# Weighted values of two pieces in one run, and the first layers' narrow products behind them, in a two-layer perceiver block

## The chip, the cores and the metric

The kernel runs on one core of a Trainium2 chip. A core has a matmul engine (PE, with its weight loads listed as PEld), a vector engine (DVE), a scalar engine (ACT), a general engine (POOL) and a queue that issues transfers (SP). The time is the device time of one execution in microseconds; the kernel before took 2208.38 us (median of three runs, 2206.98 to 2210.51).

## The reference

32 sequences `x` of 64 tokens with 256 channels each go through two layers. Each has a cross part, an attention or recurrent part and a feed-forward part. The part that matters here is the cross attention of the second layer: every sequence looks at its own context of 1601 rows.

```python
q = _split_heads(query @ Wq.T + bq)          # 16 heads of 16 channels
k = _split_heads(bank @ Wk.T + bk)
v = _split_heads(bank @ Wv.T + bv)
scores = jnp.einsum('bhqd,bhkd->bhqk', q / score_scale, k)
attn = jax.nn.softmax(scores, axis=-1)
ctx = jnp.einsum('bhqk,bhkd->bhqd', attn, v)
```

The first layer ahead of it has a product with the context's mean, a self-attention over the 64 tokens (16 heads, with a bias by distance) and a routed feed-forward; behind it come a convolution, a recurrence, a gated feed-forward and a feed-forward with rounded weights. Everything is float32, apart from a few small helpers.

## The kernel before

Two sequences make a tile of 128 rows, so there are 16 positions (`NT`). A position's context is worked off in 13 pieces (`NU`): two sequences times two halves of the channels times three pieces of 512 keys, and one piece (number 9 of 0 to 12) with the 65 last keys of both sequences. With 16 positions that is 208 pieces. `split` and `scanned` (L636, L644) say which keys piece g is; in the row scores and the keys the 65 last come first.

For a piece, PE and the others do this:

- `keys` (L671): the key projection, tile `kps`, 128x512; ACT copies it to `kt` with a bias (L692).
- `row_scores` (L713): the scores of queries by keys, tile `r`, from 32-row slices of the array; DVE reduces each of two tiles to its maxima, `mx` (L732).
- `values` (L694): the value projection `vps`; DVE copies it to one of five tiles `vau` (L709).
- `column_scores` (L752): the same scores turned round, tile `s`, with the negated maxima added through a small product (L767, L773); ACT takes the exponential into `pt` (L779).
- `weighted` (L782): `pt` times the values, accumulated over the position in one PSUM tile `o` (L797). Each product fills 32 of the array's 128 columns, and four stand next to each other.

The pieces of one position follow each other in a loop over g (L1256), whose order is written out by hand (`manual_schedule`, L1212): what is emitted first is first in each engine's queue. The order of one turn is column scores of g, values of g+4, steps of place 0, row scores of g+5, weighted values of g, keys of g+6, steps of place 1. The two score tiles of `row_scores` and the two of `column_scores` share one pool (`ps_sc`, two buffers of two banks, L57 to L66), so the column scores of the next turn take the tiles that `mx` reads. All other products share three one-bank buffers (`ps_mm`, `mm_tile`).

The other layers are generators that yield between steps. `Steps` (L1111) holds one with a stretch of turns and a number of steps, and `run(t, place)` (L1128, called from L1248) takes the steps that are due. Plans of place 3 (the first layers, `layer0`, and the second layers) run a step at place 0 if the generator last yielded `ACT`, and at place 1 otherwise. In `layer0` (L262) the products concerned are the values `v_ps` (L319, two slices of 64 columns) and the summed values `summed_values` (L381 to L388, four slices of 32 columns), which need the transposed weights `tpp` (`weights`, L369) copied to `pT` by ACT (L376).

SP loads a sequence's context into `ctxT` (two buffers) at pieces 2 and 9 of each position (L1261).

Of the kernel before, what the change touches and what calls it, by code (L numbers as in the profile page):

```python
# [9 lines left out]
F32 = mybir.dt.float32  # L10
# [5 lines left out]
P = 128  # L16
NB = 32
S = 64
# [3 lines left out]
NT = NB * S // P  # L22
# [5 lines left out]
PIECE = 512  # L28
NP = L // PIECE
TAIL = L - NP * PIECE  # L30
NU = 4 * NP + 1
# [13 lines left out]
def perceiver_kernel(ctx: ExitStack, tc: tile.TileContext, a: dict, out: bass.AP):  # L45
# [13 lines left out]


    ACT = "ACT"

    def sc_tile(name):
        return ps_sc.tile([P, 2, 512], F32, tag="sc", name=name)
# [197 lines left out]
    def layer0(ti, csum, k=0, soon=False):  # L262
# [47 lines left out]
        for oc in range(2):  # L310
            nc.gpsimd.tensor_tensor(  # L311
                kbd[oc], kT[:, oc, :].rearrange("p (b k) -> p b k", b=2).unsqueeze(2).to_broadcast([P, 2, 4, S]),
                mask4.unsqueeze(1).unsqueeze(3).to_broadcast([P, 2, 4, S]), ALU.mult)
        yield ACT
        v_ps = mm_tile([P, 2, P], f"v0_{ti}")
        for b in range(2):
            for c in range(2):
                for h in range(2):
                    nc.tensor.matmul(v_ps[h * S:(h + 1) * S, b, :], lhsT=xT[:, c, b * S:(b + 1) * S],  # L319
                                     rhs=w_v[:, c, :].rearrange("p (a h d) -> p h a d", h=2, d=16)[:, h],  # L320
                                     start=(c == 0), stop=(c == 1))
        for h in range(2):
            nc.scalar.copy(vbd[k][h * S:(h + 1) * S, :, :, h, :],
# [50 lines left out]
            return t  # L374

        def weights_out(oc, t):  # L376
            pT = tile_([P, 4, P], "pT", f"pT{oc}")
            nc.scalar.copy(pT, t)
            return pT

# [8 lines left out]

        pT = weights_out(0, weights(0))  # L390
        yield ACT
        t = weights(1)
        summed_values(0, pT)
        pT = weights_out(1, t)
        yield ACT
        summed_values(1, pT)
        yield
        o = mm_tile([P, D], f"wo_{ti}")
        mm2(o, lambda c: oT[:, c, :], lambda c: w_o[:, c, :])
# [271 lines left out]
    def keys(g):  # L671

        pos, h, k = scanned(g)
        if h is None:
            w = wholes[pos]
            w.kt = big.tile([P, 4, TAIL], F32, tag="ktr", name=f"ktr_{w.ti}", bufs=2)
            o = mm_tile([P, 2, 2 * TAIL], f"kps_{w.ti}")
            for oc in range(2):
                mm2(o[:, oc, :], lambda c: w_k2[:, c, oc * P:(oc + 1) * P],
                    lambda c: w.rest[:, c].rearrange("p b l -> p (b l)"))  # L680
            for oc in range(2):
                nc.scalar.activation(w.kt.rearrange("p (b o) l -> p o b l", o=2)[:, oc],
                                     o[:, oc, :].rearrange("p (b l) -> p b l", b=2), AF.Identity,
                                     bias=chv[:, oc, BK2:BK2 + 1])
            return
        hf = halves[h]
        kt = big.tile([P, PIECE], F32, tag="kt", name=f"kt_{hf.name}_{k}", bufs=7)
        hf.kt.append(kt)
        o = mm_tile([P, PIECE], f"kps_{hf.name}_{k}")
        cT = ctxs[hf.batch]  # L690
        mm2(o, lambda c: w_k2[:, c, hf.oc * P:(hf.oc + 1) * P], lambda c: cT[:, c, k * PIECE:(k + 1) * PIECE])
        nc.scalar.activation(kt, o, AF.Identity, bias=chv[:, hf.oc, BK2:BK2 + 1])  # L692
# [59 lines left out]
    def column_scores(g):  # L752

        pos, h, k = split(g)
        w, qbd = wholes[pos], queries[pos]
        ps = [sc_tile(f"s_{g}_{m}") for m in range(2)]
        kr = TAIL if h is None else P
        for i in range(4):
            r = slice(32 * i, 32 * i + 3)
            o = ps[i // 2][:kr, i % 2, :]  # L760
            if h is None:

                for q in range(4):
                    nc.tensor.matmul(o[:, q * P:(q + 1) * P], lhsT=onesb[r, :kr], rhs=halves[4 * pos + q].neg[r, :],
                                     start=(q == 0), stop=False)
            else:
                nc.tensor.matmul(o, lhsT=onesb[r, :], rhs=halves[h].neg[r, :].unsqueeze(1).to_broadcast([3, 4, P]),  # L767
                                 start=True, stop=False)
        for j in range(4):
            q = j if h is None else h % 4  # L770
            for i in range(4):
                r = slice(32 * i, 32 * i + 32)
                nc.tensor.matmul(ps[i // 2][:kr, i % 2, j * P:(j + 1) * P],  # L773
                                 lhsT=w.kt[r, j, :] if h is None else halves[h].kt[k][r, j * P:(j + 1) * P],
                                 rhs=qbd[r, q % 2, q // 2].rearrange("p h q -> p (h q)"), start=False, stop=(j == 3))
        w.pt[g] = []
        for m in range(2):
            pt = big.tile([P, 2, 4, P], F32, tag="pt", name=f"pt_{g}_{m}", bufs=2)
            nc.scalar.activation(pt[:kr].rearrange("p i k c -> p i (k c)"), ps[m][:kr], AF.Exp)  # L779
            w.pt[g].append(pt)  # L780

# [329 lines left out]
    class Steps:  # L1111

        def __init__(self, gen, t0=0, t1=1, n=1, place=0):
            self.gen, self.t0, self.t1, self.n, self.place, self.done = gen, t0, t1, n, place, 0
            self.kind = None
# [7 lines left out]
                    self.gen = None  # L1126

        def run(self, t, place):  # L1128
            at = place if self.place == 2 else self.place
            if self.place == 3:  # L1130
                if (self.kind == ACT) != (place == 0):
                    return
                at = place
            if at == place:
                now = t + (0.5 * place if self.place >= 2 else 0)
                while self.gen is not None and self.done * (self.t1 - self.t0) <= (now - self.t0) * self.n:
                    self.step()
                    if self.place == 3:
                        break

        def all(self):
            while self.gen is not None:
# [69 lines left out]
    with tc.manual_schedule(engines={ET.PE, ET.DVE, ET.Activation, ET.Pool}):  # L1212
        ahead, beside, summing = Steps(first()), Steps(first_layer(1, 1)), Steps(early_sums())
        early = [lambda g=g: keys(g) for g in range(1, 4)] + [lambda: keys(0)] + [
            lambda g=g: values(g) for g in range(4)] + [lambda g=g: keys(g) for g in range(4, 6)]

        def others():
            if 0 in csums:
                summing.step()
            if 1 in csums:  # L1220
                beside.step()

        ahead.step()
        late = [late_weights]
        while 0 not in queries:
            if early:
                early.pop(0)()
            ahead.step()
            others()
            if 1 in csums and late:  # L1230
                late.pop()()
        for f in early + late:
            f()
        for g in range(4):
            row_scores(g)
            others()
        maxima(0)
        row_scores(4)
        others()
        maxima_rows(0)  # L1240
        if beside.gen is not None:
            plan.insert(0, Steps(beside.gen, 0, 3, 30 - beside.done, 2))
        planned(biased(), 3, 5, 2, 1)
        if summing.gen is not None:
            plan.insert(0, Steps(summing.gen, 0, 5, 12, 0))
        planned(all_ternary(), 5, 23, 24, 2)

        def run(t, place):  # L1248
            for s in [s for s in plan if s.t0 <= t]:
                s.run(t, place)  # L1250
                if t >= s.t1 and t < NU * NT - 1:
                    s.all()
                if s.gen is None:
                    plan.remove(s)

        for g in range(NU * NT):  # L1256
            pos, p = divmod(g, NU)
            if pos + 1 < NT:
                if p == 0:
                    wholes[pos + 1].rest = load_rest(order[pos + 1])  # L1260
                if p in (2, 9):  # L1261
                    load_batch(2 * pos + 2 + p // 8)
            column_scores(g)
            if g + 4 < NU * NT:
                values(g + 4)
            if p == 0 and pos:
                normalise(pos - 1, 3)
            elif p > 3 * NP:
                normalise(pos, p - 3 * NP - 1)
            if g + 4 < NU * NT and scanned(g + 4)[2] == NP - 1:  # L1270
                maxima_rows(scanned(g + 4)[1])
            run(g, 0)
            if g + 5 < NU * NT:
                row_scores(g + 5)
                if scanned(g + 5)[2] == NP - 1:
                    maxima(scanned(g + 5)[1])
            weighted(g)
            if g + 6 < NU * NT:
                keys(g + 6)
            if p == 1 and pos:  # L1280
                x4[pos - 1] = projected(pos - 1)
            run(g, 1)
        normalise(NT - 1, 3)
        x4[NT - 1] = projected(NT - 1)
        plan.append(Steps(second_layer(NT - 1)))
        while plan:
            for s in list(plan):
                s.step()
                if s.gen is None:
                    plan.remove(s)  # L1290
# [47 lines left out]
```

## Time and profile before

| | |
|---|---|
| median of the runs | 2208.38 us |
| the profiled execution | 2210.8 us, span 2209.1 us |
| from the first column scores of the loop to the last | 91.7 to 2126.2 us |
| PE busy from 100 to 2126 us | 1961.6 of 2026 us, granted clock 0.99 |
| DVE, ACT, POOL busy in the same stretch | 1259.9, 857.1, 280.6 us |
| first 100 us: PE busy | 68.1 us, granted clock 0.78 |
| last 79 us: PE busy | 44.9 us, granted clock 0.66 |

The profile is that of one execution. Its rows give an instruction's start and length in microseconds, the engine, the line of the kernel, what it writes and reads and how many are merged into the row; in brackets the engine's idle time just before and what ended it. A matmul's record is longer than its share of the array's time, because matmuls follow each other before the first has ended, so the distance from start to start is what counts. Listed waits of an engine give the total, the number of times and the longest.

### The profile page before, as it was taken

The numbers are of one execution on the slowest core, as the hardware profiler recorded it, in microseconds if no ns is written. First come the engines' busy times: TensorE is split into PE (matmuls) and PEld (weight loads), VectorE is DVE, ScalarE is ACT, GpSimd is POOL, SyncE is SP. The second block draws the span as 40 slices with busy tenths as digits, with TensorE's granted clock in tenths as the row PEclk, the third lists the DMA queues.
The fourth block names the chain that finished last, engine by engine and source line by source line (L and its number), as shares of the span: only waits on it lengthen the run. The fifth ranks groups of instructions, "written<-read, shape, count | busy, mean of one in ns | idle before, by whom it ended". The sixth has DMA issues, their size and how long they took to land. (4 is left out here: it accounts for less than half of the span.)

```text
span 2209.1 us, 69768 instructions
## 1 busy us (share of the span) xinstructions
PE 2077.7 (94%) x31887; PEld 1520.5 (69%) x31903; DVE 1342.9 (61%) x2686; ACT 907.4 (41%) x1397; POOL 315.5 (14%) x525
## 2 busy tenths in 40 slices
PE   6799999999999999999999999999998899999984
PEld 4567677677676777777776776777776566677763
DVE  4556765666656566665665656565667656656554
ACT  3334444444435344444544444353433234334342
POOL 2111111111211111111111111111100000000011
PEclk8799999999999999999999999999999999999986
DMA  7223221111212111111211111101100101000000
GB/s 263 87 100 112 80 77 64 64 52 34 70 66 73 64 53 64 37 67 63 76 52 64 66 34 66 64 34 41 37 32 34 42 31 34 14 32 35 2 4 5
DMA packets 46175, 126.41 MB, mean 57 GB/s; under 512 B 12558, under 2 KB 28344, under 8 KB 45880
## 3 DMA queue, kind: packets, MB, share of 16 engines
q1 hardware_dynamic: 45320, 121.13, 16.0%
q8 instruction: 250, 4.10, 0.8%
q10 hardware_dynamic: 560, 0.81, 0.1%
q14 instruction: 45, 0.37, 0.1%
HBM read 119.83 MB, written 2.10 MB: 55 GB/s over the span
## 5 line engine op out<-in xcount | busy, mean ns | idle before, releaser
L779 ACT ACTIVATE pt<-s 128x1024 f32<-128x1024 f32 (+1 forms) x416 | 403.1, 1021 | 307.9 <-PE s L773 307.7
L732 DVE TENSOR_REDUCE mx<-r 128x2 f32<-128x1024 f32 x384 | 452.2, 1220 | 114.3 <-PE r L725 113.9
L233 PE MATMUL vps<-w_L_xattn_WvT,ctxT 128*128 128x128 f32 x3072 | 397.7, 283 | 0.0
L233 PE MATMUL kps<-ctxT,w_L_xattn_WkT 128*128 128x512 f32 x768 | 382.9, 622 | 11.4 <-DMA ctxT<-ctxT 11.4
L692 ACT ACTIVATE kt<-kps,chv 128x512 f32<-128x512 f32 x192 | 131.9, 687 | 636.7 <-PE kps L233 636.7
L709 DVE COPY vau<-vps 128x512 f32<-128x512 f32 (+1 forms) x208 | 143.3, 689 | 399.5 <-PE vps L233 399.5
L233 PEld LDWEIGHTS vps<-w_L_xattn_WvT,ctxT 128*128 128x128 f32 x3072 | 361.6, 193 | 24.1 <-issue 3.4
L797 PEld LDWEIGHTS o<-pt,vau 128*32 128x32 f32 (+1 forms) x13312 | 197.7, 111 | 150.9 <-issue 144.2
L797 PE MATMUL o<-pt,vau 128*32 128x64 f32 (+1 forms) x13312 | 232.3, 222 | 4.2 <-ACT pt L779 4.2
L725 PE MATMUL r<-kt,qbd 32*128 32x512 f32 x1536 | 228.5, 652 | 2.4 <-DVE mx L732 1.5
L233 PEld LDWEIGHTS kps<-ctxT,w_L_xattn_WkT 128*128 128x128 f32 x768 | 131.5, 191 | 123.0 <-issue 106.0
L773 PEld LDWEIGHTS s<-qbd,kt 32*128 32x128 f32 x6144 | 208.6, 189 | 3.2
L773 PE MATMUL s<-qbd,kt 32*128 32x128 f32 x6144 | 209.4, 273 | 0.0
L245 ACT ACTIVATE part<-part 128x1601 f32<-128x1601 f32 x60 | 92.6, 1543 | 16.2 <-DMA part<-ctxT 15.9
L725 PEld LDWEIGHTS r<-kt,qbd 32*128 32x128 f32 x1536 | 63.6, 186 | 40.8 <-issue 19.1
L767 PE MATMUL s<-neg,onesb 3*128 3x512 bf16 x768 | 80.6, 388 | 9.2 <-DVE mx L732 6.9
L767 PEld LDWEIGHTS <-onesb 3*128 3x128 bf16 x768 | 21.3, 91 | 97.6 <-issue 96.2
L815 DVE RECIPROCAL rs<-sums 128x128 f32<-128x128 f32 x64 | 60.7, 948 | 3.4 <-PE sums L812 3.3
L233 PE MATMUL ff<-nT,w_fg 128*128 128x128 f32 x384 | 51.7, 287 | 1.0 <-ACT nT L927 1.0
L311 POOL TENSOR_TENSOR kbd<-kT,mask 128x512 f32<-128x512 f32 x32 | 32.9, 1049 | 138.0 <-ACT kT L304 138.0
L233 PE MATMUL ff<-nT,w_fv 128*128 128x128 f32 x384 | 50.2, 283 | 0.0
L233 PEld LDWEIGHTS ff<-nT,w_fg 128*128 128x128 f32 x384 | 47.8, 201 | 1.9 <-ACT nT L927 1.8
(338 smaller groups left out, 2539.4 us busy)
## 6 DMA issues: line engine op xcount, KB each, us to landing
ctxT<-ctxT SPq DMA_DIRECT2D x32, 1601.0 KB, 6.9
part<-ctxT SPq DMA_DIRECT2D x60, 800.5 KB, 4.5
rest<-ctxT SPq DMA_DIRECT2D x32, 65.0 KB, 2.1
x<-x SPq DMA_DIRECT2D x16, 128.0 KB, 2.6
out<-x SPq DMA_DIRECT2D x16, 128.0 KB, 1.7
w<-w SPq DMA_DIRECT2D x16, 128.0 KB, 2.3
sum_L_ffn_w1T<-L_ffn_w1T SPq DMA_DIRECT2D x4, 256.0 KB, 6.7
raw_L_ffn_w1T<-L_ffn_w1T SPq DMA_DIRECT2D x4, 256.0 KB, 2.6
```

The source lines that it names most:

```text
L233: nc.tensor.matmul(o, lhsT=lhsT(c), rhs=rhs(c), start=(c == 0), stop=(c == 1))
L245: nc.scalar.activation(junk, src, AF.Copy, accum_out=csum[:, c, b:b + 1])
L311: nc.gpsimd.tensor_tensor(kbd[oc], kT[:, oc, :].rearrange("p (b k) -> p b k", b=2).unsqueeze(2).to_broadcast([P, 2, 4, S]), mask4.unsqueez ...
L692: nc.scalar.activation(kt, o, AF.Identity, bias=chv[:, hf.oc, BK2:BK2 + 1])
L709: nc.vector.tensor_copy(v[:kr, :, 0:VW - 16].rearrange("p k (h d) -> p k h d", d=17)[:, :, :, 0:16], o[:kr].rearrange("p k (h d) -> p k h ...
L725: nc.tensor.matmul(o, lhsT=qbd[r, q % 2, q // 2].rearrange("p h q -> p (h q)"), rhs=w.kt[r, q, :] if h is None else halves[h].kt[k][r, :], ...
L732: nc.vector.tensor_reduce(w.mx[:, 2 * m:2 * m + 2, h % 4, k], ps[m], AX.X, ALU.max)
L767: nc.tensor.matmul(o, lhsT=onesb[r, :], rhs=halves[h].neg[r, :].unsqueeze(1).to_broadcast([3, 4, P]), start=True, stop=False)
L773: nc.tensor.matmul(ps[i // 2][:kr, i % 2, j * P:(j + 1) * P], lhsT=w.kt[r, j, :] if h is None else halves[h].kt[k][r, j * P:(j + 1) * P], ...
L779: nc.scalar.activation(pt[:kr].rearrange("p i k c -> p i (k c)"), ps[m][:kr], AF.Exp)
L797: nc.tensor.matmul(w.o[32 * c:32 * c + 32, q, m, :], lhsT=v[:kr, j, 17 * hd:17 * hd + 32], rhs=pts[m][:kr, c // 2, j, c % 2 * S:c % 2 * S ...
L815: nc.vector.reciprocal(rs, t)
```

## The change

The loop takes `weighted` out of every second turn: at odd pieces it does two in a row, that of the piece before and its own, right behind the row scores; the last piece of a position (12) is done alone. Behind it stands a new place 2 for steps. `pt` has four buffers instead of two, values are emitted for g+3 instead of g+4 (the five `vau` tiles stay), `kt` has six buffers instead of seven, and the context is loaded at pieces 3 and 10.

In `layer0` the values are cut to slices of 32 columns, and both summed values go together. Both stand behind a new kind of yield, `COL`, that asks for place 2. Their second `pT` uses another tag. `Steps.run` now lets a step that is two behind its plan (three for `COL`) run at any place. One `values` moves from ahead of the loop into it.

```diff
+    COL = "COL"
...
-        yield ACT
+        yield COL
+
         v_ps = mm_tile([P, 2, P], f"v0_{ti}")
         for b in range(2):
             for c in range(2):
-                for h in range(2):
-                    nc.tensor.matmul(v_ps[h * S:(h + 1) * S, b, :], lhsT=xT[:, c, b * S:(b + 1) * S],
-                                     rhs=w_v[:, c, :].rearrange("p (a h d) -> p h a d", h=2, d=16)[:, h],
+                for j in range(4):
+                    t0 = b * S + j % 2 * 32
+                    nc.tensor.matmul(v_ps[32 * j:32 * j + 32, b, :], lhsT=xT[:, c, t0:t0 + 32],
+                                     rhs=w_v[:, c, :].rearrange("p (a h d) -> p h a d", h=2, d=16)[:, j // 2],
                                      start=(c == 0), stop=(c == 1))
...
-            pT = tile_([P, 4, P], "pT", f"pT{oc}")
+            pT = tile_([P, 4, P], "kbd" if oc else "pT", f"pT{oc}")
...
         pT = weights_out(0, weights(0))
         yield ACT
-        t = weights(1)
+        pT1 = weights_out(1, weights(1))
+        yield COL
         summed_values(0, pT)
-        pT = weights_out(1, t)
-        yield ACT
-        summed_values(1, pT)
+        summed_values(1, pT1)
...
-        kt = big.tile([P, PIECE], F32, tag="kt", name=f"kt_{hf.name}_{k}", bufs=7)
+        kt = big.tile([P, PIECE], F32, tag="kt", name=f"kt_{hf.name}_{k}", bufs=6)
...
-            pt = big.tile([P, 2, 4, P], F32, tag="pt", name=f"pt_{g}_{m}", bufs=2)
+            pt = big.tile([P, 2, 4, P], F32, tag="pt", name=f"pt_{g}_{m}", bufs=4)
...
         def run(self, t, place):
-            at = place if self.place == 2 else self.place
+            late = ((t + 0.5 * (place > 0)) - self.t0) * self.n / (self.t1 - self.t0) - self.done
             if self.place == 3:
-                if (self.kind == ACT) != (place == 0):
+                own = {None: 1, ACT: 0, COL: 2}[self.kind]
+                if place != own and late < (3 if self.kind == COL else 2):
                     return
-                at = place
-            if at == place:
-                now = t + (0.5 * place if self.place >= 2 else 0)
-                while self.gen is not None and self.done * (self.t1 - self.t0) <= (now - self.t0) * self.n:
-                    self.step()
-                    if self.place == 3:
-                        break
+            elif place == 2 or self.place != 2 and place != self.place:
+                return
+            elif self.place < 2:
+                late = (t - self.t0) * self.n / (self.t1 - self.t0) - self.done
+            while self.gen is not None and late >= 0:
+                self.step()
+                late -= 1
+                if self.place == 3:
+                    break
...
-            lambda g=g: values(g) for g in range(4)] + [lambda g=g: keys(g) for g in range(4, 6)]
+            lambda g=g: values(g) for g in range(3)] + [lambda g=g: keys(g) for g in range(4, 6)]
...
-                if p in (2, 9):
-                    load_batch(2 * pos + 2 + p // 8)
+                if p in (3, 10):
+                    load_batch(2 * pos + 2 + p // 10)
...
-            if g + 4 < NU * NT:
-                values(g + 4)
+            if g + 3 < NU * NT:
+                values(g + 3)
...
-            weighted(g)
+
+            if p % 2 or p == NU - 1:
+                for piece in range(g - p % 2, g + 1):
+                    weighted(piece)
+                run(g, 2)
```

## The prediction

> **What bounds the kernel now.** I read the page's busy shares, then the timeline of single pieces (a piece is 512 keys of one half of the channels, or the 65 last keys; 13 to a position, 208 in all), then the waits of PE.
>
> ```profile
> span 2209.1 us, 69768 instructions
> ...
> PE 2077.7 (94%) x31887; PEld 1520.5 (69%) x31903; DVE 1342.9 (61%) x2686; ACT 907.4 (41%) x1397; POOL 315.5 (14%) x525
> ...
> L732 DVE TENSOR_REDUCE mx<-r 128x2 f32<-128x1024 f32 x384 | 452.2, 1220 | 114.3 <-PE r L725 113.9
> ```
>
> PE is busy nearly always, so in the loop (about 92 to 2126 us) its work sets the time, unless a wait comes last. The reader should see the last row too: DVE takes 1.22 us for each of the two maxima reductions of a piece, and they start when PE's row scores end. Here is one piece in which PE has nothing but the fixed work:
>
> ```profile
> 1009.75 1.14 PE L725 MATMUL r<-kt,qbd 32*128 32x512 f32 x8
> ...
> 1010.82 1.10 PE L797 MATMUL o<-pt,vau 128*32 128x64 f32 x64
> 1010.92 2.36 DVE L732 TENSOR_REDUCE mx<-r 128x2 f32<-128x1024 f32 x2 [0.19 <-PE r L725]
> ...
> 1011.85 1.98 PE L233 MATMUL kps<-ctxT,w_L_xattn_WkT 128*128 128x512 f32 x4
> ...
> 1013.77 0.39 PE L767 MATMUL s<-neg,onesb 3*128 3x512 bf16 x4
> ```
>
> Start to start, PE spends 1.07 us on the row scores r, 1.03 on the weighted values o and 1.92 on the keys kps, 4.02 in all; then the column scores s write the two score tiles that the reductions read. Those end at 1010.92 + 2.36 = 1013.28, 3.53 after r began. s comes at 1013.77: DVE is 0.49 early. A piece in which DVE was late shows that s really waits:
>
> ```profile
> 212.51 1.98 PE L233 MATMUL kps<-ctxT,w_L_xattn_WkT 128*128 128x512 f32 x4
> ...
> 213.27 2.35 DVE L732 TENSOR_REDUCE mx<-r 128x2 f32<-128x1024 f32 x2
> ...
> 214.54 0.39 PE L767 MATMUL s<-neg,onesb 3*128 3x512 bf16 x2
> ...
> 215.67 0.39 PE L767 MATMUL s<-neg,onesb 3*128 3x512 bf16 x2 [0.74 <-DVE mx L732]
> ```
>
> Half of s starts, the other half stands until 0.05 after the second reduction's end (213.27 + 2.35 = 215.62). So s cannot pass 3.53 + 0.05 = 3.58 after r's start; PE's own 4.02 leaves 0.44 to spare. In the whole trace this wait is small:
>
> ```profile
> PE s L767 <- DVE mx L732: 6.9, 9, 2.2
> ```
>
> **Part 1: weighted values in pairs.** Nothing is added or dropped; o leaves every second piece ("thin") and stands doubled in the next ("thick"). A run of o is 16 groups of four matmuls, 0.06 us apart (1.10 long less the 0.22 of one matmul is 0.88 for 15 steps), so 0.90 of its 1.03 us is work and the rest the change of tile shape and back. Two in one run cost 1.03 + 0.90. A thin piece's PE work is 1.07 + 1.92 = 2.99, a thick one's 4.02 + 0.90 = 4.92. Per pair PE saves 0.13.
>
> The change of shape from r (32 rows) straight to kps (full array) is not in the loop before. Its nearest row is s to vps: s ends with about 0.10 us of drain and the first vps matmul loads its weights about 0.10 late, the same as o to kps. I take that. From both sides: free, it gains 0.2 more; as dear as both changes before, the pair saves nothing.
>
> But in a thin piece nothing covers the reductions: 2.99 of PE against 3.58. If no step of the other layers follows kps, s stands 0.59. In the order of the changed program on PE, 94 pieces have r followed by kps without o. In 39 of them a step follows (feed-forward, query or routing products, 0.35 to 2.6 us), which is cover enough but for one short one. In 55 nothing follows; in 8 of these r belongs to the 65 last keys and takes 1.85 instead of 1.07 (its reductions are 0.69 each), so they do not wait. That leaves 47 bare thin pieces and 47 covered ones.
>
> Bare pair: the thin piece goes from 4.02 to 3.58 (-0.44), the thick one +0.90: +0.46. 47 x 0.46 = **+21.6**. In the trace of before the reductions of these same 47 pieces end at 3.53 in 27, at 3.69 to 4.03 in 14 (0.33 late on average, other DVE work stands ahead), and beyond 4.3 in 6. The 14 now wait 0.33 more: **+4.6**. The 6 already waited, so their thin pieces shorten by nothing: 6 x 0.44 = **+2.6**. Covered pairs: 47 x -0.13 = **-6.3**.
>
> Two rules of the Trainium skill stand against each other here, both of the page "TensorEngine Tiling (Array Packing)". Key Properties: changing the tiling mode drains the engine. By this alone 94 pairs would gain 94 x 0.13 = 12 us, and part 2 below 9 more: about 2187. Performance Considerations, PSUM Bottleneck: tiling speeds the matmuls but not the emptying of PSUM, which may become the limit. The rows side with the second in bare pieces: r is a tiled product of 1.07 us whose emptying takes 2.36.
>
> **Part 2: first layer's column products behind them.** v (L319, 16 records on 64 columns) takes 1.02 us start to start when it stands alone before r, of which 8 x 0.112 is work; the summed values (L385) take 0.36 for 0.22 of work. Behind o the array already has 32 columns, so only the work remains. v: 14 x (0.90 - 1.02) = -1.8. Summed values: 29 runs of 0.36 become 15 of 0.45: -3.7. In the trace before, twelve of these runs also stand for a PSUM buffer or a copy (0.18 to 0.74), as here:
>
> ```profile
> 574.78 0.66 PE L373 MATMUL tpp<-ident,s 128*128 128x128 f32 x4
> 575.84 0.43 PE L385 MATMUL o<-pT,vbd 128*32 128x64 f32 x16 [0.40 <-DVE rr L896]
> ```
>
> These come to 4.0; behind o, two microseconds later, I let 3.5 go. Part 2: **-9.0**. v is now four side by side with 128 moving columns; the trace shows four side by side with 64 (o). If they took turns, v would cost 0.9 more each, +12.6; I take the reading of o. Its evacuation on ACT and the wo product behind kps have 1.9 us of kps as cover.
>
> **Part 3: the rest.** values(g+3) for values(g+4) moves one vps run (1.9 us) from the prologue, where PE was busy 68 of 100 us, into the loop: between 0 and +1.9, taken **+1**. The context load moves from piece 2 and 9 to 3 and 10 on SP's queue: it lands in 6.9 us and is first needed four pieces (about 39 us) later; the part, x and weight loads queued on SP are not tight either. Without that cover each of 30 loads would cost its 6.9. pt has four buffers, and kt six, of which five hold live keys when the next is written, so ACT's kt and exponentials wait for nothing new. Steps behind schedule may now run at another place; in the order read they stand nearly where they stood.
>
> PE also waits about 45 us in all for results of the other layers' chains (transposes for a normalised row, for example). A later PE meets some of them sooner ready: **-3**, between 0 and -12.
>
> **Sum.** 21.6 + 4.6 + 2.6 - 6.3 - 9.0 + 1 - 3 = +11.5. The profiled execution took 2210.8 us around its span of 2209.1, 2.4 over the median of the runs; it would become 2222.3, and the median 2208.4 becomes 2220.
>
> **Rivals.**
> The forecast, reductions come last in bare pieces: 2213 to 2230. Chance 0.58.
> A, faster: the stand before s is not lost, because PE meets the other chains' 45 us of waits later, and they shrink by what s stood. It decides from about 16 us absorbed on (then 11.5 + 3 - 16 is under zero); at 24 of the 29 us, 2208 - 10 = 2198. For it: those waits are spread over the same loop. Against: many need the DVE that is reducing at that time, or a matmul right before them. 0.12.
> B, no change: about half as much is absorbed, or the thin pieces' DVE is earlier than I count: 2205 to 2212. 0.14.
> C, the change of shape from r to kps costs all that was saved, so pairing saves nothing in covered pieces: 2208.4 + 11.6 + 6.3 = 2226. 0.09.
> D, the four v products take turns, or DVE falls later in the thin pieces: 2233 to 2242. 0.07.
>
> **How the numbers follow.** A measurement of this kernel can tell about 0.2% (4.4 us) from no change. Faster by more: A, 0.12. Within: B and a little of the forecast's low end, 0.15. Slower: the rest, 0.73. The range 2206 to 2233 leaves out A and D's upper part, under 0.2; it holds the bounds of the shape change and of the values, and half of v's.
>
> **What would show it.** Right: in the waits of PE, s on DVE mx rises from 6.9 us to 25 or 35, in about 50 places; in thin pieces r to s is 2.99 and half of s stands until 0.05 after the second mx; o runs of 128 matmuls are 1.9 us; L385 and v lose their own drains. Wrong: that wait stays under 15, or mx rows start earlier than 1.17 after r. The wait present and the time not longer would speak for A.

## The result and the profile after

The kernel after takes 2220.28 us (median of four runs, 2218.11 to 2222.5), the kernel before, measured with it, 2209.43 us (2206.98 to 2210.51). The ratio is 1.0051, 95% interval 1.0033 to 1.0068: slower by 10.9 us. The forecast was 2220.0, in a range of 2206 to 2233.

The profiled execution of after took 2218.11 us, span 2216.4. Its page, the lines that answer to those shown of before:

```profile
span 2216.4 us, 70294 instructions
...
PE 2071.1 (93%) x32143; PEld 1514.0 (68%) x32159; DVE 1347.1 (61%) x2686; ACT 906.9 (41%) x1397; POOL 317.2 (14%) x525
...
L735 DVE TENSOR_REDUCE mx<-r 128x2 f32<-128x1024 f32 x384 | 452.2, 1220 | 90.2 <-PE r L728 89.7
```

PE is busy 6.6 us less and the span is 7.3 us longer. DVE does the same reductions in the same time. So PE stands more, and the waits of PE in after say for what:

```profile
PE s L770 <- DVE mx L735: 22.4, 46, 1.5
...
PE o L389 <- issue: 5.0, 3, 3.4
...
PE o L800 <- issue: 2.5, 1, 2.5
...
PE v L323 <- issue: 1.4, 2, 0.9
```

Two things have grown. The column scores wait for the maxima 46 times instead of 9. And the idle times that end with "issue", which means that PE waited for nothing that the profile shows, make 10.3 us in the whole trace where before has 1.8, nearly all of it in one row:

```profile
PE s L773 <- issue: 1.4, 1, 1.4
```

The first was forecast, the second was not.

The first can be read in one thin piece (r at 1012.65) and the thick one after it (r at 1022.77), from the timeline of after:

```profile
1012.65 1.14 PE L728 MATMUL r<-kt,qbd 32*128 32x512 f32 x8
...
1013.72 1.98 PE L235 MATMUL kps<-ctxT,w_L_xattn_WkT 128*128 128x512 f32 x4
1013.83 2.36 DVE L735 TENSOR_REDUCE mx<-r 128x2 f32<-128x1024 f32 x2 [0.19 <-PE r L728]
...
1015.64 0.39 PE L770 MATMUL s<-neg,onesb 3*128 3x512 bf16 x2
...
1016.24 0.39 PE L770 MATMUL s<-neg,onesb 3*128 3x512 bf16 x2 [0.21 <-DVE mx L735]
...
1022.77 1.14 PE L728 MATMUL r<-kt,qbd 32*128 32x512 f32 x8
...
1023.84 1.99 PE L800 MATMUL o<-pt,vau 128*32 128x64 f32 x128
1023.94 2.36 DVE L735 TENSOR_REDUCE mx<-r 128x2 f32<-128x1024 f32 x2 [1.17 <-PE r L728]
...
1025.76 1.99 PE L235 MATMUL kps<-ctxT,w_L_xattn_WkT 128*128 128x512 f32 x4
...
1027.68 0.40 PE L770 MATMUL s<-neg,onesb 3*128 3x512 bf16 x4
```

Thin piece: r to s is 1015.64 - 1012.65 = 2.99. The reductions end at 1013.83 + 2.36 = 1016.19, and the second half of s starts 0.05 later, at 1016.24. The row prints only 0.21 of idle time, because the record of the first half is 0.39 long; from half to half it is 0.60. Thick piece: 128 matmuls of o take 1.92 from start to start, all four rows of s go at once, and the 1.38 us that DVE is early are worth nothing.

Counted from half to half over the loop, s stands 53 times for 37.9 us in after, and 19 times for 8.4 us in before.

### The profile page after: what moved, and what is told of

Read it like the earlier page. It is cut to its first block, busy times and chain, and to the rows that moved or that the text cites. A ratio compares the mean times of both kernels' runs of the same rounds, so it can differ in the third digit from the quotient of the medians.

```text
span 2216.4 us, 70294 instructions
## 1 busy us (share of the span) xinstructions
PE 2071.1 (93%) x32143; PEld 1514.0 (68%) x32159; DVE 1347.1 (61%) x2686; ACT 906.9 (41%) x1397; POOL 317.2 (14%) x525
## 5 line engine op out<-in xcount | busy, mean ns | idle before, releaser
L735 DVE TENSOR_REDUCE mx<-r 128x2 f32<-128x1024 f32 x384 | 452.2, 1220 | 90.2 <-PE r L728 89.7
L800 PEld LDWEIGHTS o<-pt,vau 128*32 128x32 f32 (+1 forms) x13312 | 192.3, 110 | 88.2 <-issue 86.0
L776 PE MATMUL s<-qbd,kt 32*128 32x128 f32 x6144 | 217.1, 272 | 0.9 <-issue 0.8
L800 PE MATMUL o<-pt,vau 128*32 128x64 f32 (+1 forms) x13312 | 210.9, 220 | 4.1 <-issue 2.5
L770 PE MATMUL s<-neg,onesb 3*128 3x512 bf16 x768 | 95.4, 385 | 25.5 <-DVE mx L735 22.4
```

What stands on the lines that cost most here:

```text
L735: nc.vector.tensor_reduce(w.mx[:, 2 * m:2 * m + 2, h % 4, k], ps[m], AX.X, ALU.max)
L800: nc.tensor.matmul(w.o[32 * c:32 * c + 32, q, m, :], lhsT=v[:kr, j, 17 * hd:17 * hd + 32], rhs=pts[m][:kr, c // 2, j, c % 2 * S:c % 2 * S ...
```

## The experiments

Two theories stood at the start. **R**: the loss is the stand of the column scores in bare thin pieces. **F**: the loss is PE standing for its instructions. Two more (C and Q) came with the last four kernels. Each ratio is against the kernel before as measured with the same group: 2209.92 us (11 runs) for the first four kernels, 2206.93 us (27 runs) for the last four.

### Pairs alone

The changed kernel with `layer0` as before:

```diff
-        yield COL
+        yield ACT
...
-        pT1 = weights_out(1, weights(1))
-        yield COL
+        t = weights(1)
         summed_values(0, pT)
-        summed_values(1, pT1)
+        pT = weights_out(1, t)
+        yield ACT
+        summed_values(1, pT)
```

(and the values in two slices of 64 columns again).

> Pairing alone; the first layers' values and summed values stand where and as they stood before. 43 bare thin pieces are left in PE's order (46 with the whole change). Theory R (the reductions come last in bare thin pieces): the waits of the column scores on mx stay at about 45 and 33 us counted from score record to score record, and without the 9 us of the narrow products the time is 2227 to 2231. Theory F (the loss sits in gaps in which PE waits for nothing shown, nine with 10.3 us in the changed kernel against three with 1.8 before, each behind an instruction packet of queue 8, and the longer runs of narrow products bring them): fewer narrow products in a row, so gaps fall to about 3 us and the time is 2211 to 2215.

2232.68 us (2221.14 to 2239.55), ratio 1.0103, 1.0076 to 1.0129. F falls: neither the time nor the gaps came down (idle times without a cause: 7.4 us, not 3). R is met within the interval, but the six runs spread by 18 us: they follow the mean granted clock, from 0.975 at 2221 us to 0.967 at 2239, so the size of this part is known less well than that of the others. The two runs at 0.975, the clock of after's profiled execution, took 2221.14 and 2223.61, which is 11 to 14 us over before and under R's range. The profiled execution is the slowest of the six: in its loop 30.2 us of clock are withheld (one minus the granted share, summed over time), in that of before 17.2. In its profile s stands 53 times for 36.5 us, nearly as in after.

### Narrow products alone

The changed kernel with the loop as before (weighted values in each turn, values for g+4, buffers and loads as they were):

```diff
-            if p % 2 or p == NU - 1:
-                for piece in range(g - p % 2, g + 1):
-                    weighted(piece)
-                run(g, 2)
+            weighted(g)
+            run(g, 2)
```

> The narrow products alone: values in 32-column slices and both summed values behind the weighted values, which are done every turn as before; buffers, value order and loads as before. Theory R: PE's work falls by 6 and its waits at the summed values by 3, no thin pieces, so 2198 to 2203. Theory F: the runs of narrow products are what costs, so 2207 or more.

2193.45 us (2186.83 to 2194.82), ratio 0.9924, 0.9910 to 0.9938. F falls again. It is even better than R expected: -16.5 us, where the prediction's term for this part was -9.0. Its waits of PE have the column scores where before had them:

```profile
PE s L770 <- DVE mx L735: 6.7, 10, 2.2
```

### The reductions cut in half, in both kernels

The maxima are taken over the first 256 of the 512 keys, in after and in before:

```diff
-nc.vector.tensor_reduce(w.mx[:, 2 * m:2 * m + 2, h % 4, k], ps[m], AX.X, ALU.max)
+nc.vector.tensor_reduce(w.mx[:, 2 * m:2 * m + 2, h % 4, k], ps[m][:, :, 0:256], AX.X, ALU.max)
```

> The changed kernel with the maxima taken over the first 256 of each 512 keys alone (the rest is left out of the maxima, the softmax is still divided by its own sum). A reduction then takes about 0.65 us instead of 1.22, and both end about 2.5 us after the row scores begin, ahead of a thin piece's 2.99. Theory R: the 37 us of standing before the column scores go almost wholly, 2220 to about 2183, and it ends 8 to 18 us under the kernel before with the same halving. Theory F or any cause elsewhere: it falls only as far as the kernel before does with the halving, about 8 to 10 us, to 2210.

> The kernel before with the same halved maxima, as the control. All theories: only its 8 us of standing before the column scores can go, and a few us where DVE came late for other steps: 2197 to 2203.

After with half reductions: 2175.56 us (2171.74 to 2176.32), ratio 0.9846, 0.9833 to 0.9859. Before with half reductions: 2192.16 us (2189.89 to 2194.62), ratio 0.9926, 0.9911 to 0.9942. With a reduction of 686 ns in place of 1220 the same change makes the kernel 16.6 us faster instead of 10.9 slower. The reductions and the waits of PE in the first of the two:

```profile
L735 DVE TENSOR_REDUCE mx<-r 128x2 f32<-128x512 f32 x384 | 247.4, 686 | 90.0 <-PE r L728 89.4
```

```profile
PE o L389 <- issue: 4.2, 2, 3.2
PE s L770 <- DVE mx L735: 3.0, 7, 1.0
...
PE o L800 <- issue: 2.2, 1, 2.2
```

The wait for the maxima is nearly gone (10 stands, 4.3 us from half to half), and the idle times without a cause are nearly as large as in after (9.1 us in all). They cost something, but the sign of the result hangs on the length of the reductions. F, as the cause of the sign, is out. This pair of kernels does not say which wait of DVE it is; the next experiment does. Both kernels came out lower than expected. Before, too, gains 17.8 us from faster reductions: s stood for 8.4 us there, and the listed waits of PE for other chains in the loop fell from 53.8 to 50.7 us; where the rest comes from is not shown.

### Pairs only where something covers the reductions

In the 46 bare thin pieces a piece's weighted values go behind its own keys; the rest of the change stays:

```diff
+            before = len(products)
             run(g, 1)
+            if held and len(products) == before and p != 3 * NP - 1 and g + 5 < NU * NT:
+                weighted(held.pop())
```

(`held` is the piece whose weighted values are still owed; `products` lists the PSUM tiles that steps have asked for.)

> The changed kernel, but a piece without weighted values gets its own back, behind the keys, wherever no step of another layer follows those keys (46 bare pieces); its partner then does one run of o, not two. All other pairs and the narrow products behind them stay. Theory R (the loss is the stand of the column scores in bare pieces): their standing falls from 37.9 us to about 9, 46 pairs lose their 0.13 us again (+6), and half of the instruction gaps goes with half of the double runs (-4): 2190 to 2198, below both kernels. Theory C (pairing itself costs, whatever follows the keys): half of the pairs remain, so half of the loss remains: 2203 to 2210.

2195.70 us (2191.95 to 2201.8), ratio 0.9950, 0.9933 to 0.9967. R holds, C falls. The piece shown above, from the timeline of this kernel, and its line in the waits of PE:

```profile
1007.67 1.14 PE L731 MATMUL r<-kt,qbd 32*128 32x512 f32 x8
...
1008.74 1.98 PE L238 MATMUL kps<-ctxT,w_L_xattn_WkT 128*128 128x512 f32 x4
1008.84 2.36 DVE L738 TENSOR_REDUCE mx<-r 128x2 f32<-128x1024 f32 x2 [0.19 <-PE r L731]
...
1010.65 1.10 PE L803 MATMUL o<-pt,vau 128*32 128x64 f32 x64
...
1011.69 0.40 PE L773 MATMUL s<-neg,onesb 3*128 3x512 bf16 x4
```

```profile
PE s L773 <- DVE mx L738: 6.1, 8, 2.2
```

The reductions end at 1011.20, s comes at 1011.69, 0.49 later, as it was before the change. s stands 22 times for 9.3 us in all. The buffers, the values for g+3 and the later loads of the change are all still there, so they are not the loss. One part of the expectation missed: the idle times without a cause stayed at 8.6 us instead of falling by half. This kernel and the narrow part alone both beat the two kernels; between themselves they cannot be told apart (2191.95 to 2201.8 against 2186.83 to 2194.82, in different groups).

### The two runs of a pair set apart

The thick piece does o, keys, o:

```diff
-                for piece in range(g - p % 2, g + 1):
-                    weighted(piece)
-                run(g, 2)
-            if g + 6 < NU * NT:
-                keys(g + 6)
+                if p % 2:
+                    weighted(g - 1)
+                if g + 6 < NU * NT:
+                    keys(g + 6)
+                weighted(g)
+                run(g, 2)
+            elif g + 6 < NU * NT:
+                keys(g + 6)
```

> The changed kernel with the two runs of weighted values of a pair set apart by the keys; the pieces without any stay without. Theory Q (the gaps in which PE waits for nothing shown come from 256 and more narrow instructions issued in one stretch): gaps over 0.15 us fall from 9 with 10.3 us to about 3 with 2 to 3 us; the second change of tile shape comes back (94 x 0.13 = +12), the stand of the column scores stays (38 us): 2222 to 2227. Rival (the gaps belong to the whole number of instructions or to chance): they stay at 8 to 10 us, and the time is 2230 to 2235.

2235.66 us (2232.51 to 2237.2), ratio 1.0122, 1.0106 to 1.0138. Split verdict. The gaps did what Q says: in the waits of PE the row of o L800 falls from 2.5 to 0.2 and that of o L389 from 5.0 to 1.5, and all idle times without a cause from 10.3 to 2.5 us.

```profile
PE s L770 <- DVE mx L735: 21.9, 46, 1.5
...
PE o L389 <- issue: 1.5, 1, 1.5
...
PE o L800 <- issue: 0.2, 1, 0.2
```

But the time is 15 above after and not 4, because I had priced the parting by one change of tile shape. Start to start, kps takes 1.82 ahead of another product on the full array, 1.91 ahead of o and 1.92 ahead of s. So where a step follows, parting costs (1.03 + 1.91 + 1.03) - (1.92 + 1.82) = 0.23 a pair, and 0.14 only where s follows: about 63 x 0.23 + 30 x 0.14 = 18.7 in place of 12. With 7.9 less of gaps and 2.1 more of other waits this makes 12.9 of the 14.0 us that the loop grew against after.

### The rule for late steps alone, and the values alone

The kernel before with the new `Steps.run`; and the narrow part with the summed values as they were:

```diff
-            if self.place == 3:
-                if (self.kind == ACT) != (place == 0):
-                    return
-                at = place
+            if self.place == 3:
+                own = {None: 1, ACT: 0, COL: 2}[self.kind]
+                if place != own and late < (3 if self.kind == COL else 2):
+                    return
```

> The kernel before with one thing of the change: a step of the other layers that is two behind its plan runs at either place. The prediction took this as nothing: within 3 us of the kernel before (2207 to 2213), other waits of PE in the loop at 50 to 57 us. Rival (this rule is what makes the narrow part gain 16.5 instead of the 9 predicted): 2200 to 2203, other waits near 46.

> The narrow part alone (weighted values in every turn) with the summed values as they were: two runs apart, before the row scores. By the prediction's terms it keeps the 1.8 us of the values and loses the 3.7 and 3.5 of the summed values: about 7 above the whole narrow part, 2199 to 2203. Rival (the surplus of the narrow part sits in the values and the rule for late steps): 2194 to 2197. Other rival (all of it sits in the summed values): 2206 to 2210.

The rule alone: 2209.12 us (2199.78 to 2212.12, 21 runs), ratio 1.0006, 0.9998 to 1.0013: nothing, as the prediction took it. The values alone: 2200.27 us (2198.88 to 2201.74), ratio 0.9967, 0.9955 to 0.9978, in the expected place; so the values are worth 6.7 us and the summed values about 9 or 10 more. In the trace of the values alone, PE's other waits in the loop are 48.9 us and not 53.8. That is 4.9 of the 6.7, and leaves about the 1.8 us of drains that the prediction gave the values.

## Why the prediction was right, step by step

**The 3.58 and the 0.59.** Right to the hundredth: 2.99 from r to s, 0.60 of standing, 0.05 after the second reduction. The steps behind it hold as well: r to kps directly costs what r to o did (last r to first kps 0.517 against 0.518), so rival C of the prediction is out.

**How many and how long.** The order has 46 bare thin pieces with a full r and nine of the 65 last keys, not 47 and eight. In terms of standing alone the prediction had 47 x 0.59 + 4.6 + 2.6 = 34.9 us more; measured are 37.9 - 8.4 = 29.5. The excess is in the terms for a late DVE. (The covered pairs, 47 x -0.13, are -6.1 and not -6.3, and 14 x (0.90 - 1.02) is -1.7 and not -1.8: 0.3 us, which does not matter.) The forecast of "25 to 35 us in the waits of PE" was put in the wrong view: that list counts only the idle time behind the end of the first half's record and shows 22.4.

**Work of PE.** 94 pairs at -0.13, the drains of v and L389 and the moved values made -16.7; counted over the loop from start to start it is -19.3, and -21.3 if the shortest distance of each kind of neighbours is taken throughout, so it is known to about 2 us. v behind o takes 0.90 plus 0.09, so four products do stand side by side, and the taking of turns in rival D is out.

**Other waits.** The prediction took -3.5 and -3.0. The listed idle time of these waits in the loop fell by 11.4 us, from 53.8 to 42.3. But the loop is 14.7 longer (2034.5 to 2049.3), and work, standing and the gaps below (8.7 of them in the loop) make -19.3 + 29.5 + 8.7 = 18.9. If these three are right, only 4.2 of the 11.4 arrive. Up to 3.0 of what is missing is clock: 20.2 us are withheld in the loop of after, 17.2 in that of before. One place of it is behind the longest gap, where the first kps takes 2.91 and not 1.98 (see the last section). The rest is in places that I can't separate.

**What no step had: +8.5 us** of idle time without a cause (1.8 in before, 10.3 in after), see the last section. It was offset by the ends of the execution: the first s comes 3.9 us earlier and the part behind the last s is 3.6 shorter. The first is not the moved values, as the prediction would have it: the four other kernels with the same move start their loop between 87.5 and 93.5 us, the four others without it between 88.9 and 95.1. It goes with the granted clock of the first 100 us: 0.83 in after, 0.78 in before, 0.81 in the kernel that starts at 87.5 and 0.75 in the two that start at 95.0 and 95.1. So 14.7 - 3.9 - 3.6 = 7.2, the 7.3 us of the spans. Before's profiled execution lies 1.4 over its median and after's 2.2 under, which makes the 10.9 of the medians.

**Part 2.** -9.0 in the sum; alone it is -16.5. About 5 of the difference are waits of other chains that the values save; the summed values are worth between 2 and 3 more than taken, and where is not shown. Alone, the parts make +22.8 and -16.5, together 6.3, and the whole is 10.9. But at a clock of 0.975 the pairs alone took 2221.14 and 2223.61 us and the whole 2218.11, so behind the pairs the narrow products seem to be worth 3 to 6 us, far less than alone. One reason can be seen: the same waits of other chains can be saved only once (6.7 us by one part, 7.5 by the other, 11.4 by both). How much less is open, because the size of the pairs is.

So the mechanism and its size are shown: the half reductions turn +10.9 into -16.6, which is 27.5 us, and the covered pairs take 28.6 us of standing away and end 24.6 us lower. But the exact hit of the total is partly luck, since the standing was 5 us under its term, the gaps 8.5 over, and the ends of the execution offset what remained. Rival A, that the wait would be there but absorbed, fails: it needed 16 us from other waits, and only 11.4 are listed as gone.

The rule of the Trainium skill in "TensorEngine Tiling (Array Packing)", Performance Considerations, PSUM Bottleneck, is borne out: a tiled product is over in 1.07 us and its emptying takes 2.36; with emptying at 686 ns a tile the change gains 16.6 us instead. That the other rule, by which each change of mode drains the array, is what then decides is not shown: the narrow products gain as much alone, with the long reductions, and whatever the 94 pairs save does not show in the total; idle times without a cause, 9.1 us against 1.2 in the other kernel with half reductions, take back 7.9 of it.

## What to carry to other kernels

Before work is moved to save an engine a change of mode, add up what it covered at its old place: here 1.03 us of products were worth moving for 0.13, but they hid 0.59 of a reduction. Moving them only where something else covers that wait takes the loss away (2195.70 us against 2220.28). That the moved products then gain anything is not shown: the kernel without any pairs is as fast. And when two parts of a change can be run apart, price and run each alone: the narrow products alone were worth 16.5 us, and the pairs took more than that away.

## What was not expected of the hardware

PE can stand although all its data is there. The longest such place, from the timeline of after:

```profile
687.85 2.00 PE L800 MATMUL o<-pt,vau 128*32 128x64 f32 x128
...
689.46 0.34 SPq L97 DMA_DIRECT2D part<-ctxT  x1
...
689.66 0.62 PE L389 MATMUL o<-pT,vbd 128*32 128x64 f32 x30
...
693.67 0.27 PE L389 MATMUL o<-pT,vbd 128*32 128x64 f32 x2 [3.38 <-issue]
...
693.87 2.91 PE L235 MATMUL kps<-ctxT,w_L_xattn_WkT 128*128 128x512 f32 x4
```

PE had done 158 narrow matmuls, each with its weight load, in 2.4 us when it stopped in the middle of a run, and went on 3.38 us later with the same tiles. A look at the same stretch by microseconds (length, then busy time of PE, PEld, DVE, ACT and POOL, granted clock, share of the DMA engines, GB/s):

```profile
688.00:689.00 1.00, 1.00 (x81) 1.00 (x79) 1.00 (x1) 1.00 (x1) 0.00 (x0) 1.00 1.01 423
689.00:690.00 1.00, 1.00 (x86) 1.00 (x79) 1.00 (x2) 0.44 (x2) 0.00 (x0) 1.00 1.01 423
690.00:691.00 1.00, 0.29 (x21) 0.13 (x11) 0.78 (x2) 0.37 (x1) 0.00 (x0) 1.00 0.94 391
691.00:692.00 1.00, 0.00 (x0) 0.00 (x0) 0.00 (x0) 0.00 (x0) 0.00 (x0) 1.00 0.70 209
692.00:693.00 1.00, 0.00 (x0) 0.00 (x0) 0.00 (x0) 0.00 (x0) 0.00 (x0) 1.00 0.84 275
...
694.80:698.20 3.40, 3.40 (x11) 1.68 (x10) 0.00 (x0) 0.69 (x1) 0.00 (x0) 0.50 0.05 14
```

The stop costs more than its own length. The granted clock is 1.00 while PE stands, and 0.50 for 3.4 us from 694.8 on, and the kps that runs into it takes 2.91 us. Of the eight idle times of this kind over 2 us in all traces, seven are followed by 3.4 us at half clock, 3.0 to 4.5 us after PE stopped.

About 160 instructions a microsecond go through, while a context transfer fills the DMA engines. The page lists a queue for instructions, with packets of 16 KB:

```profile
q8 instruction: 252, 4.13, 0.8%
```

In after, all eight idle times of this kind over 0.15 us in the loop have such a packet that starts 2.2 to 2.7 us ahead of PE's going on (here at 691.33); in the ten traces together it is so for all 38, with 2.2 to 2.9 us. The two longest, 3.38 and 2.53 us, fall where the DMA engines are full, as do the other six over 2 us. Parting the double runs takes most of it away (10.3 to 2.5 us). That narrow instructions are used up faster than they are fetched, the more so beside a large transfer, fits all of this. It is not shown beyond that: in the kernel with covered pairs the same places kept their gaps with half of the double runs, so where a packet's end happens to fall matters as well. The Trainium skill ("Runtime: NRT & Kernel Launch", Instruction fetch mechanics) has the instructions fetched ahead in blocks of 16 KiB, at a cost mostly hidden; in the kernel before that holds (1.4 us in the loop), in after less so (10.1).
